# Softplus summed by TensorE in its bank, and one more output product on VectorE, in a fused conv, selective-scan and attention kernel

## The chip, the cores and the metric

The kernel runs on one core of a Trainium2 chip. A core has five engines with in-order instruction streams of their own: TensorE (matmuls into the PSUM banks), VectorE, ScalarE, GpSimd and SyncE, which issues the DMAs here. In the profile they are PE (and PEld, its weight loads), DVE, ACT, POOL and SP. The metric is the device time of one launch in microseconds, the median of several runs.

## What is computed

Eight images of 96 channels and 64 x 64 points go through a layer norm, an input projection, a depthwise convolution, a selective scan over four orders of the points, a gated output projection, a small convolutional branch, linear attention and a quantized feed-forward. Most of the time goes to the selective scan, and the change lies there. Cut to it:

```python
x_dbl = jnp.einsum('bkdl,kcd->bkcl', xs, x_proj_w)             # k: 4 orders, l: 4096 points
dts, bs, cs = (x_dbl[:, :, :R], x_dbl[:, :, R:R + N], x_dbl[:, :, R + N:])   # R = 6, N = 16
dts = jnp.einsum('bkrl,kdr->bkdl', dts, dt_projs_w)            # d: 192 channels
delta = jax.nn.softplus(dts + dt_projs_b[None, :, :, None])
A = -jnp.exp(A_logs)
...
def step(hst, inp):
    u_i, dt_i, b_i, c_i = inp
    dA = jnp.exp(dt_i[..., None] * A)
    hst = dA * hst + (dt_i * u_i)[..., None] * b_i[:, :, None, :]
    y = jnp.einsum('bkdn,bkn->bkd', hst, c_i)
    return (hst, y)
```

For each order, channel d and state n there is a linear recurrence over the 4096 points. `delta` is called the step size.

## The kernel before

**Units.** The scan is cut into 256 units: 8 images x 4 orders x 8 chunks of 512 points, in that order. A unit has six tiles (`TILES`: g in 0, 1 and j in 0 to 2), and each tile has four states (`G`), so 24 slots. In a slot 128 partitions hold 64 channels times two states. The 192 channels are three groups j of 64.

**A slot.** The decay `exp(delta * A)` is made by ScalarE into a PSUM bank (`decays`, three banks of tag "da", two slots ahead). VectorE then runs one scan instruction (L1145) with the decay and the input product as operands, and it starts from the last value that the same state had in the chunk before (`carry`). In a *banked* slot the scan's result goes back to the decay's bank and VectorE multiplies it with C into the tile `hb` (L1147, the product with C); ScalarE copies the last value into `carry` (L1148). In the other slots the scan's result goes to `hb` in place; GpSimd multiplies with C later for all such states of the tile at once (`outputs`, L965), after ScalarE's copy of their last values to `carry` (L1153). `BANKED` tells how many states of each of the six tiles are banked: 4, 0, 4, 0, 4 and then 1 or 2. The first eight units of images 1 to 7 have 1 (13 banked states in the unit), all others 2 (14).

**The inputs.** GpSimd multiplies `b` with `du` = delta x u, a whole tile of 4 x 512 at a time (`inputs`, L959), two tiles ahead of the scan. `b`, `c`, `delta` and `du` are spread from a compact form to the 128 partitions by DMAs on SP (`states`, `spread`).

**The step sizes.** `step_sizes(us, i)` has six steps for one tile `nat` of 128 x 512. Step 0: TensorE forms dts @ dt_w + bias in the single PSUM bank of tag "dt" (L924). Step 1: ScalarE writes the absolute value to `nat` (L932). Step 2: exp(-nat) (L934). Step 3: ln(1 + nat) (L936). Step 4: VectorE adds max(bank, 0) to it (L938), which is the softplus. Step 5: GpSimd multiplies with u, to give du (L941). There are 384 such chains: one for the first 128 channels of each unit (called the a-chain here, 256), and one for the last 64 channels of two units together, in odd units (the pair's or b-chain, 128).

**The sums over states.** TensorE sums the products with C over the states, and the two halves of the partitions, by a matmul with `halves` into the banks "y01" and "y2" (`sums`, L985), adds the skip term or earlier orders by an identity matmul (L994), and ScalarE copies the banks out (`gather`, L1004 and L1007).

**The order.** All engines' streams are written out by hand: `plan` gives for each unit the work put into each of its 24 slots, and every call there appends to the engines' in-order streams in the order of the slots and, inside a slot, of the `put` calls. At the end of each slot one step of the *side streams* may be appended: the front of the next image (normalization, projection, convolution) and the back end of the image before (gating, convolutions, attention, feed-forward). These are generators that yield a number of slots between an operation and the next one that needs its result; `CALM` lists slots in which they may swap ScalarE's function tables.

In `plan`, before: the a-chain of the unit after next has steps 0, 1, 2 in slots 20, 22, 23, and steps 3, 4, 5 follow in slots 0, 2, 4 of the next unit; its spreads are in slots 4 (delta) and 6 (du). The b-chain has steps 0 to 4 in slots 9, 11, 12, 13, 15 and step 5 in slot 16 of odd units, with spreads in slots 17 and 18 (and, for the second unit of the pair, 15 and 16 of the unit after).

Of the kernel before, what the change touches and what calls it, by code (L numbers as in the profile page):

```python
# [12 lines left out]
AF = mybir.ActivationFunctionType  # L13
ALU = mybir.AluOpType
# [7 lines left out]
DI, N, R = 192, 16, 6  # L22
T = 512
NC = L // T
# [6 lines left out]
SPREAD = 5  # L31
HB = 6

BANKED = ((4, 0, 4, 0, 4, 1), (4, 0, 4, 0, 4, 2))

HOLD = 3
LAND = 11
# [6 lines left out]
def kernel(ctx: ExitStack, tc: tile.TileContext, a, out):  # L44
# [8 lines left out]
    nc = tc.nc  # L53
# [9 lines left out]
    def bank(tag, name):  # L63
        return psum.tile([P, T], F32, tag=tag, name=name, bufs=BANKS[tag])


    ident = wp.tile([P, P], F32, name="ident")
# [39 lines left out]
    def into(t, src):  # L107
        nc.sync.dma_start(t, src)
        return t
# [13 lines left out]
    def load(name, shape):  # L123
        return into(wp.tile(shape, F32, name="w_" + name), a[name])
# [26 lines left out]
    dt_w = wp.tile([P, 3, 64], F32, name="dt_w")  # L151
    for k in range(4):
        into(dt_w[32 * k : 32 * k + R], a["dt_w"][:, k, :, 0:64])
        into(dt_w[32 * k + R : 32 * k + R + 1], a["dt_b"][0:64, k, :].rearrange("p j -> j p").unsqueeze(0))
    dt_w = dt_w.rearrange("r j d -> r (j d)")
    a_neg = load("a_logs", [P, 4, 3, 8])
    nc.scalar.activation(a_neg, a_neg, AF.Exp)
# [698 lines left out]
    for b in range(out.shape[0]):  # L856

        s = {"b": b, "done": set(), "live": b + 1 == out.shape[0], "pairs": (1, 0) if b else (0, 1)}
        images.append(s)
        for order, (pair, back) in enumerate((p, k) for p in s["pairs"] for k in range(2)):  # L860
            for i in range(NC):
                u = Unit()
                u.s, u.pair, u.back, u.k = s, pair, back, pair + 2 * back
                u.c, u.start = (NC - 1 - i if back else i), i == 0
                u.order, u.new, u.i = order, (order, i) == (0, 0), len(units)
                u.bc, u.hb, u.delta, u.du = {}, {}, {}, {}
                u.banked = BANKED[int(b == 0 or u.i % 32 >= NC)]
                units.append(u)

    TILES = [(g, j) for g in range(2) for j in range(3)]  # L870
# [32 lines left out]
    def fetched_u(u):  # L903

        u.ua = sp.tile([P, T], F32, tag="ua", name="ua", bufs=1)
        nc.sync.dma_start(u.ua, u.s["u"][u.pair][0:P, bass.ts(u.c, T)])
# [6 lines left out]

    def step_sizes(us, i):

        u, which = us[0], "ab"[len(us) - 1]
        if i == 0:
            u.ps = bank("dt", "dt")
            if which == "a":
                todo = [(u.ps, slice(0, P), u)]  # L920
            else:
                todo = [(u.ps[64 * h : 64 * h + 64], slice(P, DI), w) for h, w in enumerate(us)]
            for ps, d, w in todo:
                nc.tensor.matmul(ps, dt_w[32 * w.k : 32 * w.k + R + 1, d], w.dts, start=True, stop=True)  # L924
            u.nat = sp.tile([P, T], F32, tag="nat" + which, name="nat", bufs=1)
            if which == "a":
                u.nata = u.nat
            else:
                for w in us:
                    w.natb = u.nat  # L930
        elif i == 1:
            nc.scalar.activation(u.nat, u.ps, AF.Abs)  # L932
        elif i == 2:
            nc.scalar.activation(u.nat, u.nat, AF.Exp, scale=-1.0)  # L934
        elif i == 3:
            nc.scalar.activation(u.nat, u.nat, AF.Ln, bias=one)  # L936
        elif i == 4:
            nc.vector.scalar_tensor_tensor(u.nat, u.ps, 0.0, u.nat, ALU.max, ALU.add)  # L938
        else:
            x = u.ua if which == "a" else u.ub  # L940
            nc.gpsimd.tensor_tensor(x, u.nat, x, ALU.mult)  # L941
# [73 lines left out]
    def plan(u, last, nxt, third):  # L1015

        at = [[] for _ in range(24)]

        def put(slot, f, *args):
            at[slot].append((f, args))  # L1020

        if last:
            put(0, outputs, last, 5)
            put(0, before, last)
            for m in range(2):
                put(m, sums, last, (3, 4), 2 + m)
            for m in range(2):
                put(5 + m, sums, last, (5,), m)
            put(7, states, u, 1, 1)
            put(10, gather, last, 0)  # L1030
            put(11, gather, last, 1)
        for n in range(6):
            to = (u, n + 2) if n < 4 else (nxt, n - 4)
            if to[0]:
                put(4 * n + 1, inputs, *to)
        if third and u.i % 2:
            put(16, step_sizes, (nxt, third), 5)
        put(8, outputs, u, 1)
        put(16, outputs, u, 3)
        for m in range(4):  # L1040
            put(13 + m, sums, u, (0, 1), m)
            if m < 2:
                put(18 + m, sums, u, (2,), m)
                put(22 + m, sums, u, (3, 4), m)
        if nxt:
            for i, slot in enumerate((0, 2, 4)):
                put(slot, step_sizes, (nxt,), i + 3)
            put(4, spread, nxt, 0, (0, 1))
            put(6, spread, nxt, 1, (0, 1))
            put(10, states, nxt, 0, 0)  # L1050
            put(15, states, nxt, 1, 0)
            put(20, states, nxt, 0, 1)
            if u.i % 2 == 0:
                put(15, spread, nxt, 0, (2,))
                put(16, spread, nxt, 1, (2,))
        if third:
            put(1, fetched_dt, third)
            put(9, fetched_u, third)
            for i, slot in enumerate((20, 22, 23)):
                put(slot, step_sizes, (third,), i)  # L1060
            if u.i % 2:
                for i, slot in enumerate((9, 11, 12, 13, 15)):
                    put(slot, step_sizes, (nxt, third), i)
                put(17, spread, nxt, 0, (2,))
                put(18, spread, nxt, 1, (2,))
            elif u.i + 3 < len(units):
                put(21, fetched_pair, third, units[u.i + 3])
        return at

    def at_index(i):  # L1070
        return units[i] if 0 <= i < len(units) else None
# [22 lines left out]
    for what in range(2):  # L1094
        spread(units[0], what, range(3))
    fetched_u(units[1])
    for i in range(3):
        step_sizes(units[1:2], i)
    inputs(units[0], 0)
    inputs(units[0], 1)  # L1100
# [9 lines left out]
    for u in units:  # L1110
        last, nxt, third = (at_index(u.i + d) for d in (-1, 1, 2))
        if u.new:
            drained(*side)
            b = u.s["b"]
# [16 lines left out]
        if u.start:  # L1131
            carry = sp.tile([P, 24], F32, tag="carry", name="carry")
        todo = plan(u, last, nxt, third)
        for slot in range(24):
            n, m = divmod(slot, G)
# [6 lines left out]
            d = da.pop(q)  # L1142
# [105 lines left out]
```

## Time and profile before

| what | us |
|---|---|
| median of 3 runs | 11,285.59 |
| lowest and highest run | 11,276.82, 11,286.57 |
| the profiled execution | 11,276.69 |
| its span, first to last instruction | 11,274.7 |
| first scan starts, last scan ends | 299, 11,036 |
| mean of one unit in that stretch | 41.94 |

The costliest groups of that execution:

| line, engine | what | count | mean ns |
|---|---|---|---|
| L959 POOL | input product, 128 x 2048 | 1536 | 4535 |
| L965 POOL | output product, four states | 512 | 4528 |
| L941 POOL | step size times u | 384 | 1279 and 1277 |
| L1145 DVE | scan, 128 x 512 | 6144 | 1204 to 1280 |
| L1147 DVE | product with C, 128 x 512 | 3528 | 692 |
| L938 DVE | softplus sum, 128 x 512 | 384 | 676 |
| L1080 ACT | decay, 128 x 512 | 6144 | 689 |
| L932, L934, L936 ACT | Abs, Exp, Ln of a chain | 384 each | 587, 617, 709 |
| L985 PE | sum over states, records | 12,288 | 724 |
| L924 PE | dt product, records | 1024 | 677 and 647 |

How to read it: a row's mean is one instruction's duration, and neighbours on an engine overlap a little, so the distance from one start to the next is shorter than the sum of durations. A matmul of 32-bit operands shows as two records. An engine's share of busy time averages over stages; which engine sets the pace is read from who waits for whom.

### The profile page before, as it was taken

The page shows a single profiled execution, that of the slowest core. Times are in us where ns is not written, and L with a number is a line of the kernel's source. Part 1 is how long each engine was busy: PE and PEld are TensorE (multiplying, and loading weights), DVE is VectorE, ACT ScalarE, POOL GpSimd, SP SyncE. Part 2 cuts the span into 40 slices and gives each one's busy share as a digit, 9 for nine tenths or more (in the row PEclk, how much of TensorE's full clock was granted, in tenths as well). Part 3 has the DMA queues.
Part 4 walks back from the last instruction along what each step waited for, and adds up shares of the span by engine and source line. Part 5 has one row for each costly group of instructions (what it writes and reads, how often), then busy time and mean ns, then how long its engine had stood idle before and what let it go on. Part 6 is the DMA issues. An engine that isn't in the chain of part 4 may idle for free. (4 is left out here: it accounts for less than half of the span.)

```text
span 11274.7 us, 97032 instructions
## 1 busy us (share of the span) xinstructions
PE 8525.3 (76%) x23270; PEld 2313.7 (21%) x23270; DVE 10391.9 (92%) x10868; ACT 7482.6 (66%) x14899; POOL 10398.6 (92%) x2782
## 2 busy tenths in 40 slices
PE   6677668887788877888678886788767887676677
PEld 1121112222122211222112221222212221111112
DVE  0999999999999999999999999999999999999993
ACT  2666666767666676667766676666766667666674
POOL 0999999999999999999999999999999999999991
PEclk8787778888788877889788887888878887777778
DMA  3788888988888888888888888889888888888883
GB/s 76 195 200 196 200 190 208 215 219 203 199 208 214 217 194 210 208 210 219 195 208 212 213 215 193 217 200 226 209 199 209 213 221 199 194 198 196 202 201 91
DMA packets 1095376, 2253.25 MB, mean 200 GB/s; under 512 B 435993, under 2 KB 436698, under 8 KB 963731
## 3 DMA queue, kind: packets, MB, share of 16 engines
q1 hardware_dynamic: 1094803, 2247.05, 82.1%
q8 instruction: 184, 3.01, 0.1%
q14 instruction: 389, 3.19, 0.1%
HBM read 1507.14 MB, written 336.69 MB: 164 GB/s over the span
## 5 line engine op out<-in xcount | busy, mean ns | idle before, releaser
L959 POOL TENSOR_TENSOR hb<-b,du 128x2048 f32<-128x2048 f32 x1536 | 6938.6, 4535 | 27.0 <-DMA du<-ua 17.0
L1080 ACT ACTIVATE da<-delta,w_a_logs 128x512 f32<-128x512 f32 x6144 | 4216.2, 689 | 693.1 <-DVE hb L1145 570.8
L985 PE MATMUL p<-hb,halves 128*64 128x512 f32 x12288 | 3788.4, 724 | 787.4 <-POOL hb L965 368.5
L1145 DVE TENSOR_TENSOR_SCAN da<-da,carry,hb 128x512 f32<-128x512 f32 x3087 | 3950.2, 1280 | 52.8 <-ACT da L1080 48.9
L965 POOL TENSOR_TENSOR hb<-hb,c 128x2048 f32<-128x2048 f32 (+2 forms) x768 | 2984.6, 3886 | 296.8 <-ACT carry L1153 252.9
L1145 DVE TENSOR_TENSOR_SCAN hb<-da,carry,hb 128x512 f32<-128x512 f32 x2289 | 2781.6, 1265 | 63.6 <-ACT da L1080 62.6
L1147 DVE TENSOR_TENSOR hb<-da,c 128x512 f32<-128x512 f32 x3528 | 2440.8, 692 | 153.9 <-DVE da L1145 0.5
L1148 ACT COPY carry<-da 128x1 f32<-128x1 f32 x3528 | 554.8, 157 | 2337.9 <-DVE hb L1147 2327.3
L985 PEld LDWEIGHTS p<-hb,halves 128*64 128x64 f32 x12288 | 911.3, 161 | 3513.9 <-issue 2095.9
L435 PE MATMUL conv<-f0im,taps 97*128 97x512 f32 (+1 forms) x2088 | 913.0, 670 | 93.3 <-ACT f0pre L491 54.0
L1145 DVE TENSOR_TENSOR_SCAN da<-da,hb 128x512 f32<-128x512 f32 x441 | 537.7, 1219 | 28.3 <-POOL hb L959 27.3
L941 POOL TENSOR_TENSOR ua<-nat,ua 128x512 f32<-128x512 f32 x256 | 327.4, 1279 | 203.0 <-DMA ub<-u 203.0
L924 PE MATMUL dt<-dts,dt_w 7*64 7x512 f32 (+1 forms) x1024 | 451.1, 662 | 15.8 <-DVE nat L938 12.6
L994 PE MATMUL p<-u,ident 128*128 128x512 f32 x768 | 436.2, 695 | 8.8 <-DMA u<-y 8.8
L938 DVE SCALAR_TENSOR_TENSOR nat<-dt,nat 128x512 f32<-128x512 f32 x384 | 259.6, 676 | 184.4 <-ACT nat L936 184.4
L435 PEld LDWEIGHTS conv<-f0im,taps 97*128 97x128 f32 (+1 forms) x2088 | 256.2, 175 | 683.5 <-issue 523.9
L1145 DVE TENSOR_TENSOR_SCAN hb<-da,hb 128x512 f32<-128x512 f32 x327 | 377.9, 1204 | 4.9 <-ACT da L1080 4.9
L376 PE MATMUL ctr<-f1e,cen_c 96*96 96x512 f32 x402 | 234.7, 693 | 137.4 <-DVE f1e L770 98.6
L382 PE MATMUL var<-f1e,ones_c 96*96 96x512 f32 x350 | 210.8, 687 | 146.3 <-ACT f1e L379 131.7
L619 PE MATMUL cab<-f1im,cab_w 97*32 97x512 f32 x1044 | 272.3, 642 | 14.7 <-DVE f1pad L598 7.8
L1153 ACT COPY carry<-hb 128x4 f32<-128x4 f32 (+2 forms) x768 | 146.8, 191 | 196.1 <-DVE hb L1145 184.1
L656 PE MATMUL cab<-f1m,cab_w 96*96 96x512 f32 x348 | 205.2, 717 | 93.1 <-ACT f1e L665 42.1
(427 smaller groups left out, 7512.6 us busy)
## 6 DMA issues: line engine op xcount, KB each, us to landing
b<-xd SPq DMA_DIRECT2D x1024, 512.0 KB
c<-xd SPq DMA_DIRECT2D x1024, 512.0 KB
delta<-nat SPq DMA_DIRECT2D x1536, 128.0 KB
du<-ua SPq DMA_DIRECT2D x1024, 128.0 KB
y<-yt SPq DMA_DIRECT2D x512, 256.0 KB
u<-y SPq DMA_DIRECT2D x384, 256.0 KB
ua<-u SPq DMA_DIRECT2D x256, 256.0 KB
du<-ub SPq DMA_DIRECT2D x512, 128.0 KB
```

The lines of the kernel that those rows point to most:

```text
L435: nc.tensor.matmul(ps, taps[:, t, lo : lo + n], im[:, r0 + dy : r0 + dy + 8, dx : dx + HW], start=t == 0, stop=t == 8,)
L619: nc.tensor.matmul(ps[at : at + 32, :], cab1_w[:, t, :], k.im.t[:, 8 * q + dy : 8 * q + dy + 8, dx : dx + HW], start=t == 0, stop=t == 8, ...
L924: nc.tensor.matmul(ps, dt_w[32 * w.k : 32 * w.k + R + 1, d], w.dts, start=True, stop=True)
L941: nc.gpsimd.tensor_tensor(x, u.nat, x, ALU.mult)
L959: nc.gpsimd.tensor_tensor(hb, u.bc[0, g], u.du[j].unsqueeze(1).to_broadcast([P, G, T]), ALU.mult)
L965: nc.gpsimd.tensor_tensor(hb, hb, u.bc[1, TILES[n][0]][:, lo:, :], ALU.mult)
L985: nc.tensor.matmul(ps, halves, u.hb[n][:, i, :], start=TILES[n][0] == 0 and m == 0, stop=False, skip_group_check=True)
L994: nc.tensor.matmul(ps, w, x, start=False, stop=True, skip_group_check=True)
L1080: nc.scalar.activation(da[q], u.delta[j], AF.Exp, scale=a_neg[:, u.k, j, g * G + m : g * G + m + 1])
L1145: nc.vector.tensor_tensor_scan(dd if banked else x, dd, x, 0.0 if u.start else col, ALU.mult, ALU.add)
L1147: nc.vector.tensor_tensor(hb[:, m, :], d, u.bc[1, g][:, m, :], ALU.mult)
L1148: kept.append(lambda col=col, d=d, at=first_at: nc.scalar.copy(col, d[:, at : at + 1]))
```

## The change

The chain's bank holds half of the pre-activation, since `dt_w` (weights and bias) is scaled by 0.5 at the start. After the absolute value, TensorE adds `nat` to the bank by an identity matmul, so that the bank holds max(x, 0). The exponential takes a scale of -2. After the logarithm TensorE adds `nat` again, and the bank holds the softplus; ScalarE copies it to `nat` in step 4, which was VectorE's. `BANKED` becomes 2 for the first eight units of images 1 to 7 and for all even units, and 3 for the other odd units: 14 or 15 banked states. The steps are put into other slots: of the a-chain, 0 and 1 into slots 18 and 20, 2 to 5 into slots 0, 1, 3, 5 of the next unit, spreads 5 and 7; of the b-chain, 0 to 4 into slots 7, 8, 10, 11, 16, step 5 into 17, spreads 18 and 19.

```diff
-BANKED = ((4, 0, 4, 0, 4, 1), (4, 0, 4, 0, 4, 2))
+BANKED = ((4, 0, 4, 0, 4, 2), (4, 0, 4, 0, 4, 3))
...
+        half_w = dt_w[32 * k : 32 * k + R + 1]
+        nc.vector.tensor_scalar(half_w, half_w, 0.5, None, ALU.mult)
...
-                u.banked = BANKED[int(b == 0 or u.i % 32 >= NC)]
+                u.banked = BANKED[u.i % 2 if b == 0 or u.i % 32 >= NC else 0]
...
+        def added():
+            nc.tensor.matmul(u.ps, ident, u.nat, start=False, stop=True, skip_group_check=True)
...
         elif i == 1:
             nc.scalar.activation(u.nat, u.ps, AF.Abs)
+            added()
         elif i == 2:
-            nc.scalar.activation(u.nat, u.nat, AF.Exp, scale=-1.0)
+            nc.scalar.activation(u.nat, u.nat, AF.Exp, scale=-2.0)
         elif i == 3:
             nc.scalar.activation(u.nat, u.nat, AF.Ln, bias=one)
+            added()
         elif i == 4:
-            nc.vector.scalar_tensor_tensor(u.nat, u.ps, 0.0, u.nat, ALU.max, ALU.add)
+            nc.scalar.copy(u.nat, u.ps)
...
+        if nxt:
+            for i, slot in ((2, 0), (3, 1), (4, 3), (5, 5)):
+                put(slot, step_sizes, (nxt,), i)
+        if third and u.i % 2:
+            put(17, step_sizes, (nxt, third), 5)
...
-        if third and u.i % 2:
-            put(16, step_sizes, (nxt, third), 5)
...
-            for i, slot in enumerate((0, 2, 4)):
-                put(slot, step_sizes, (nxt,), i + 3)
-            put(4, spread, nxt, 0, (0, 1))
-            put(6, spread, nxt, 1, (0, 1))
+            put(5, spread, nxt, 0, (0, 1))
+            put(7, spread, nxt, 1, (0, 1))
...
-            for i, slot in enumerate((20, 22, 23)):
+            for i, slot in enumerate((18, 20)):
                 put(slot, step_sizes, (third,), i)
             if u.i % 2:
-                for i, slot in enumerate((9, 11, 12, 13, 15)):
+                for i, slot in enumerate((7, 8, 10, 11, 16)):
                     put(slot, step_sizes, (nxt, third), i)
-                put(17, spread, nxt, 0, (2,))
-                put(18, spread, nxt, 1, (2,))
+                put(18, spread, nxt, 0, (2,))
+                put(19, spread, nxt, 1, (2,))
...
-    for i in range(3):
+    for i in range(2):
         step_sizes(units[1:2], i)
```

More of the change, by code (lines that the diff above doesn't have):

```diff
@@ L923, in step_sizes @@
             for ps, d, w in todo:
-                nc.tensor.matmul(ps, dt_w[32 * w.k : 32 * w.k + R + 1, d], w.dts, start=True, stop=True)
+                nc.tensor.matmul(
+                    ps, dt_w[32 * w.k : 32 * w.k + R + 1, d], w.dts, start=True, stop=True, skip_group_check=True
+                )
             u.nat = sp.tile([P, T], F32, tag="nat" + which, name="nat", bufs=1)
```

## The prediction

> **What bounds the kernel now.** I read the busy shares first, then the shares by stretch, then the waits of the two busiest engines, then single instructions in order of time. The chain that ended last adds up to only a few per cent of the span, so it names no bound here. The page:
>
> ```profile
> PE 8525.3 (76%) x23270; PEld 2313.7 (21%) x23270; DVE 10391.9 (92%) x10868; ACT 7482.6 (66%) x14899; POOL 10398.6 (92%) x2782
> ```
>
> VectorE and GpSimd tie at 92%, start and end included. The two stretches below are image 0 and images 1 to 7 of the scan loop (stretch, length, then PE, PEld, DVE, ACT, POOL busy with counts, granted clock, DMA share, GB/s).
>
> ```profile
> 300.00:1590.00 1290.00, 888.32 (x2348) 240.48 (x2350) 1250.69 (x1271) 818.48 (x1648) 1278.03 (x336) 0.78 0.82 196
> 1590.00:11030.00 9440.00, 7281.56 (x19989) 1952.99 (x19986) 9058.60 (x9422) 6483.37 (x12977) 9092.94 (x2412) 0.83 0.85 207
> ```
>
> In image 0 GpSimd is busy 99%, VectorE 97%; in the rest both are at 96%. The waits between 450 and 10,900 us decide between them (us in total, times, longest):
>
> ```profile
> DVE hb L1145 <- ACT da L1080: 67.5, 93, 3.0
> DVE da L1145 <- ACT da L1080: 48.9, 22, 6.4
> ...
> DVE f1ln L719 <- ACT var L370: 24.2, 22, 2.7
> ...
> DVE da L1145 <- POOL hb L959: 4.9, 7, 1.2
> ```
>
> ```profile
> POOL hb L965 <- ACT carry L1153: 233.7, 193, 4.3
> POOL ub L941 <- DVE nat L938: 51.7, 38, 3.2
> ```
>
> VectorE waits 4.9 us for GpSimd; GpSimd waits 233.7 us for carry copies, which themselves wait for the last scan of a tile. So VectorE sets the pace after image 0, and GpSimd is close behind. VectorE's other stalls are late decays: ScalarE is in order, and a decay stuck behind other work holds a scan up.
>
> **What one instruction is worth on VectorE** is a distance between starts, not a duration:
>
> ```profile
> 5019.84 1.23 DVE L1145 TENSOR_TENSOR_SCAN hb<-da,hb 128x512 f32<-128x512 f32 x1 [0.76 <-ACT da L1080]
> 5020.98 1.27 DVE L1145 TENSOR_TENSOR_SCAN da<-da,carry,hb 128x512 f32<-128x512 f32 x1
> 5022.33 0.69 DVE L1147 TENSOR_TENSOR hb<-da,c 128x512 f32<-128x512 f32 x1
> 5022.94 1.28 DVE L1145 TENSOR_TENSOR_SCAN da<-da,carry,hb 128x512 f32<-128x512 f32 x1
> ...
> 5026.79 0.68 DVE L938 SCALAR_TENSOR_TENSOR nat<-dt,nat 128x512 f32<-128x512 f32 x1
> 5027.39 1.28 DVE L1145 TENSOR_TENSOR_SCAN da<-da,carry,hb 128x512 f32<-128x512 f32 x1
> ```
>
> A slot with the product takes 1.96 us here, and the softplus sum adds 0.60 (5026.79 to 5027.39). Over all 6144 scans the mean from scan to scan is 1.942 us with a product, 1.210 without; with a softplus sum between, 2.527 and 1.785. So a product costs 0.73 us and a softplus sum 0.58. As a test: 3528 x 1.942 + 2616 x 1.210 + 384 x 0.58 = 10,240 us of a loop of 10,737 (first scan 299, last end 11,036); the other 500 are the side streams' products and their stalls.
>
> **The change on VectorE.** Removed: 384 softplus sums (L938) x 0.58 = 223 us. Added: products. Before, 56 units had 13 and 200 had 14 (3528). After, the 56 have 14, 100 even ones 14, 100 odd ones 15: 3684, so 156 more x 0.73 = 114 us. Net 109 us less, all on the pacing engine, about 0.85 us per pair of units. Four tiny scalings of dt_w run at the start, where VectorE is busy 17.9 of the first 200 us: nothing; if that cover were gone, four small instructions, under 2 us.
>
> **On GpSimd.** The output product of the last tile loses one state 156 times. The rows:
>
> ```profile
> L965 POOL TENSOR_TENSOR hb<-hb,c 128x1024 f32<-128x1024 f32 x200 | 473.0, 2365 | 111.4 <-ACT carry L1153 95.3 <-DMA ub<-u 4.3 <-DMA x1d<-f1e 3.2
> L965 POOL TENSOR_TENSOR hb<-hb,c 128x1536 f32<-128x1536 f32 x56 | 193.1, 3447 | 7.5 <-DMA u<-u 3.7 <-ACT carry L1153 3.0
> ```
>
> A state is 3447 - 2365 = 1.08 us, so 168 us less. That is more than VectorE's 109, so GpSimd does not take over. In image 0, where it is full, it gives back 16 x 1.08 = 17 us against VectorE's 16 x 1.03 = 16 (3 x 0.58 - 0.73 per pair). Against this, step 5 (the product with u, one per chain) now waits for ScalarE's copy in slot 3 instead of VectorE's sum in slot 2. GpSimd began it in slot 3 in 138 of 256 units; the copy ends some 1.45 us into slot 3 (carry 0.16 + decay 0.69 + copy 0.58), the sum ended just as it began. At worst 138 x 1.4 = 190 us of new GpSimd wait, at best none; images 1 to 7 have 9440 - 9093 = 347 us of GpSimd idle time to hide it, so I take 8 us. The pair's product moves past one output product (slot 16 to 17), and its two du transfers from slot 18 to 19; their first reader is in slot 1 of the next unit, 6 slots on. The a-chain's four delta and four du issues go from slots 4 and 6 to 5 and 7 on SP; their readers are in slots 17 and 22. SP already waits there (on nat, 1917 us in all) without holding anyone: nothing; if the cover went, the next issue behind them (b, c) has 5 slots.
>
> **On ScalarE** each chain gains one copy out of the bank, and each matmul chain two adds on TensorE. The nearest rows:
>
> ```profile
> L1007 ACT COPY yt<-p 128x512 f32<-128x512 f32 x368 | 212.5, 578 | 6.6 <-PE p L994 6.6
> L994 PE MATMUL p<-u,ident 128*128 128x512 f32 x768 | 436.2, 695 | 8.8 <-DMA u<-y 8.8
> ```
>
> Copies: 384 x 0.578 = 222 us, ScalarE from 66 to 69%. It lies beside VectorE as long as decays stay ahead. From the times in the trace, a decay ends 1.1 to 3.5 us (medians by slot) before its scan, except in odd units' slots 14 and 15, where it is 0.4: there the pair's chain runs its Exp and Ln in slots of 1.2 us. Slots 13 to 16 of odd units run 0.63 us over their medians, 128 x 0.63 = 80 us. The change moves this chain to slots 8, 10, 11 and 16, where a slot lasts 1.9 us, and the other chain's Abs and Exp from 22 and 23 to 20 and 0. The stall of decays may thus shrink, at most by those 80 us.
>
> **On TensorE**, 384 x 2 adds by the identity, two records each. L994 is the same shape: in order of time a lone pair of such records takes 1.10 us (four take 1.98), so 768 x 1.10 = 845 us at most, 768 x 0.99 = 760 in a row; the share goes from 76 to about 83%. No term of the path, but three waits are new: the add waits for Abs (or Ln) and holds every later matmul, the side streams' and sums among them; Exp waits until the add has read nat; the copy waits for the second add. Behind Exp and the copy on ScalarE stand the decays. From Abs to Exp there are 4 slots (a-chain) or 2 (b-chain), from Ln to the copy 2 or 5. ScalarE's cover is the lead above; bounds: nothing, and 2 x 1.10 x 384 = 845 us if every one were felt. With 180 us of ScalarE waiting for TensorE in the loop today over more than a thousand hand-overs, I take 5 to 10% of 845, about 60, and against it most of the 80 of the emptied slots: zero for both together, ends -70 and +60.
>
> [...] Here waits on TensorE reach 11 us, and the granted clock was 0.78 in image 0 and 0.83 in the busier rest. [...]
>
> **Sum.** The profiled execution took 11,276.7 us (span 11,274.7). 11,276.7 - 109 + 8 + 0 = 11,176; the median of the three runs is 8.9 above that execution, so 11,185 us, -0.9%. Its own range, from -70 to +60: 11,115 to 11,245.
>
> **Rivals.**
> *More than that (0.12).* The 80 us of odd slots 13 to 16 vanish and TensorE costs nothing: 11,185 - 75 = 11,110. For it: the 0.4 us lead there. Against: even units, with no pair chain, run over in the same slots too.
> *GpSimd keeps half (0.10).* It waits for the copy in every unit where it came early and falls behind: of the 190 us a third shows, 11,185 + 55 = 11,240. For: 99% in image 0. Against: 347 us of idle time later.
> *It does nothing, within 0.2% (0.08).* The 109 us are eaten by late decays, 11,285.
> *Slower (0.20).* ScalarE in order: Exp in slots 0 and 10, Abs in 8 (one slot after its matmul, where there were two) and the copy in slots 3 and 16 wait for a TensorE that is itself held by the adds, and decays come late. Priced 845 us times the share VectorE feels; it decides from (109 - 8) / 845 = 12%, and at a fifth it is 169 us: 11,354. For: 83% TensorE, an odd unit with five such ScalarE steps besides the decays in slots 8 to 11. Against: TensorE began the dt product slots ahead of its place in half the units.
>
> **How the numbers follow.** Forecast 0.50. What a measurement here can tell from no change is about 0.2%, 23 us. Faster: 0.50 + 0.12 + 0.10 = 0.72; same 0.08; slower 0.20. From 11,090 (5% below) to 11,320 (a share of 16% felt, some 12% above).
>
> **What would show it.** No VectorE row of nat; L1147's row at 3684, VectorE's scan to scan at 1.94 and 1.21 as now; GpSimd 168 us less busy; "DVE L1145 <- ACT da" not above 180 us; odd slots 13 to 16 shorter. Wrong if ScalarE's waits for PE dt exceed 100 us, or VectorE's for ScalarE double.

## The result, and the profile after

The changed kernel takes 11,366.82 us (median of four runs, 11,366.36 to 11,383.9) against 11,282.42 for the kernel before on the same chip: a ratio of 1.0079, 95% interval 1.0061 to 1.0096. It is 84 us slower where 100 us faster was forecast, and outside the range; the rival "Slower" had named 11,354. The profiled execution took 11,367.25 us, its span is 11,365.5.

The page's row of busy times:

```profile
PE 9025.4 (79%) x24806; PEld 2505.5 (22%) x24806; DVE 10279.0 (90%) x10644; ACT 7712.2 (68%) x15439; POOL 10235.4 (90%) x2782
```

The two engines that tied have both less to do: VectorE 113 us less than before, GpSimd 163. So the work went away as forecast, and the time went up. The two stretches of the scan loop (stretch, length, PE, PEld, DVE, ACT, POOL busy with counts, granted clock, DMA share, GB/s) show where:

```profile
300.00:1590.00 1290.00, 942.12 (x2545) 258.75 (x2544) 1238.01 (x1242) 855.64 (x1721) 1269.18 (x337) 0.83 0.82 196
1590.00:11110.00 9520.00, 7707.29 (x21316) 2119.49 (x21312) 8951.57 (x9216) 6672.93 (x13437) 8939.64 (x2411) 0.87 0.84 205
```

In images 1 to 7 VectorE and GpSimd fell from 96% to 94% each: neither is full, and something else holds both up. Image 0 became 8.7 us shorter (1292.9 to 1284.2 from first scan to first scan of image 1); the loss is in the rest. The waits between 450 and 11,000 us (us in total, times, longest) name it:

```profile
PE dt L924 <- ACT nat L944: 598.6, 206, 8.9
PE dt L924 <- ACT nat L949: 370.7, 173, 7.7
PE dt L924 <- ACT carry L1163: 329.9, 117, 8.0
...
ACT nat L944 <- PE dt L934: 184.6, 88, 9.0
DVE hb L1160 <- ACT da L1095: 96.4, 133, 2.8
DVE da L1160 <- ACT da L1095: 93.1, 53, 6.1
...
ACT nat L952 <- PE dt L924: 18.2, 23, 2.8
...
DVE da L1160 <- POOL hb L973: 1.1, 3, 0.5
```

L924 is the add, L934 the dt product, L944 Abs, L947 Exp, L949 Ln, L952 the copy, L1160 the scan, L1095 the decay. TensorE stands before its adds for 1,300 us, waiting for Abs or Ln (a carry copy, L1163, is named where it was the last thing on ScalarE to signal). Such a wait of TensorE before an add is called a hold below. ScalarE's Abs now waits 185 us for the dt product; before it was this:

```profile
ACT nat L932 <- PE dt L924: 2.7, 2, 2.0
```

Most of that comes from the new slots and not from the adds: a kernel below with the new slots and no add has 146.5 us of it. VectorE's waits for decays went from 116 to 190 us. GpSimd does not pace it: VectorE waits 1.1 us for it. The same in groups of instructions (count, then busy and mean ns, then idle time before them and its releasers):

```profile
L924 PE MATMUL dt<-nat,ident 128*128 128x512 f32 x1536 | 1097.0, 803 | 1348.1 <-ACT nat L944 611.6 <-ACT nat L949 383.4 <-ACT carry L1163 343.9
L944 ACT ACTIVATE nat<-dt 128x512 f32<-128x512 f32 x384 | 223.9, 583 | 208.7 <-PE dt L934 196.3 <-DMA delta<-nat 11.7 <-DMA b<-xd 0.2
L947 ACT ACTIVATE nat<-nat 128x512 f32<-128x512 f32 x384 | 237.8, 619 | 5.2 <-PE dt L924 5.1
L952 ACT COPY nat<-dt 128x512 f32<-128x512 f32 x384 | 222.0, 578 | 25.5 <-PE dt L924 25.0
L1162 DVE TENSOR_TENSOR hb<-da,c 128x512 f32<-128x512 f32 x3684 | 2547.7, 692 | 181.6 <-DMA c<-xd 12.5 <-DVE da L1160 1.8 <-issue 0.9
```

Of the new hand-overs that the forecast named, Exp (5.1 us) and the copy (25 us) hardly wait; the adds do. VectorE's product now waits 12.5 us for the transfer of c. One stretch of an odd unit shows a whole chain. First TensorE in order of time (start, duration, engine, line, operation; in brackets the idle time before it and its releaser):

```profile
6680.67 1.02 PE L924 MATMUL dt<-nat,ident 128*128 128x512 f32 x2
6681.53 1.02 PE L437 MATMUL conv<-f0im,taps 97*128 97x512 f32 x2
6682.40 0.38 PE L781 MATMUL ff<-f1x,q_w 96*128 96x512 fp8e5 x1
6682.61 1.02 PE L437 MATMUL conv<-f0im,taps 97*128 97x512 f32 x2
6689.69 2.07 PE L924 MATMUL dt<-nat,ident 128*128 128x512 f32 x2 [6.05 <-ACT carry L1163]
6691.56 1.91 PE L437 MATMUL conv<-f0im,taps 97*128 97x512 f32 x2
6693.40 1.97 PE L999 MATMUL p<-hb,halves 128*64 128x512 f32 x4
6695.30 0.39 PE L781 MATMUL ff<-f1x,q_w 96*128 96x512 fp8e5 x1
```

Then ScalarE, and VectorE:

```profile
6687.81 0.69 ACT L1095 ACTIVATE da<-delta,w_a_logs 128x512 f32<-128x512 f32 x1 [2.96 <-DVE hb L1160]
...
6688.92 0.72 ACT L949 ACTIVATE nat<-nat,one 128x512 f32<-128x512 f32 x1
...
6691.45 1.90 ACT L1095 ACTIVATE da<-delta,w_a_logs 128x512 f32<-128x512 f32 x3
6695.73 0.58 ACT L789 CAST f1h<-ff 128x512 f16<-128x512 f32 x1 [2.38 <-PE ff L781]
...
6697.63 0.69 ACT L1095 ACTIVATE da<-delta,w_a_logs 128x512 f32<-128x512 f32 x1
```

```profile
6696.64 0.69 DVE L1162 TENSOR_TENSOR hb<-da,c 128x512 f32<-128x512 f32 x1
6698.35 1.29 DVE L1160 TENSOR_TENSOR_SCAN da<-da,carry,hb 128x512 f32<-128x512 f32 x1 [1.02 <-ACT da L1095]
```

The pair's second add reaches the head of TensorE's stream at 6683.6 and stands there for 6.05 us, until Ln ends on ScalarE (6688.92 + 0.72). Ln itself is that late because it stands behind a decay that waits 2.96 us for a scan. Nothing behind the add passes it. The convolution, the sums and a feed-forward matmul (L781) follow, the add and the first of these in about twice the time (2.07 and 1.91 us where the same pairs took 1.02). ScalarE comes to the copy of that feed-forward bank and waits 2.38 us; the decay behind it comes late, and a scan waits 1.02 us. ScalarE holds TensorE, TensorE holds ScalarE, and VectorE pays.

How much it pays can be counted: idle gaps of VectorE over 60 ns in images 1 to 7 add up to 458 us before and 647 after (both hold about 175 behind the last scan). The 189 more are 14 in even units and 175 in odd ones, which have the pair's chain. By what the profile names as their end, 81 of them stand before scans and 61 before VectorE's other steps, both for ScalarE, 19 for TensorE and 17 for a transfer: late decays are less than half, and the side streams' steps most of the rest. With the forecast's -109 that makes +80; measured was +84.

### The profile page after: what moved, and what is told of

The parts are those of the page before. It is cut to its first block, busy times and chain, and to the rows that moved or that the text cites. A ratio compares the mean times of both kernels' runs of the same rounds, so it can differ in the third digit from the quotient of the medians.

```text
span 11365.5 us, 99689 instructions
## 1 busy us (share of the span) xinstructions
PE 9025.4 (79%) x24806; PEld 2505.5 (22%) x24806; DVE 10279.0 (90%) x10644; ACT 7712.2 (68%) x15439; POOL 10235.4 (90%) x2782
## 5 line engine op out<-in xcount | busy, mean ns | idle before, releaser
L1095 ACT ACTIVATE da<-delta,w_a_logs 128x512 f32<-128x512 f32 x6144 | 4208.1, 690 | 790.8 <-DVE hb L1160 667.3
L1160 DVE TENSOR_TENSOR_SCAN da<-da,carry,hb 128x512 f32<-128x512 f32 x3236 | 4138.8, 1279 | 99.5 <-ACT da L1095 96.9
L999 PE MATMUL p<-hb,halves 128*64 128x512 f32 x12288 | 3540.8, 683 | 224.3 <-ACT yt L1021 128.0
L979 POOL TENSOR_TENSOR hb<-hb,c 128x2048 f32<-128x2048 f32 (+2 forms) x768 | 2818.2, 3670 | 408.8 <-ACT carry L1168 327.8
L1162 DVE TENSOR_TENSOR hb<-da,c 128x512 f32<-128x512 f32 x3684 | 2547.7, 692 | 181.6 <-DMA c<-xd 12.5
L1160 DVE TENSOR_TENSOR_SCAN hb<-da,carry,hb 128x512 f32<-128x512 f32 x2140 | 2608.9, 1265 | 90.2 <-ACT da L1095 82.5
L924 PE MATMUL dt<-nat,ident 128*128 128x512 f32 x1536 | 1097.0, 803 | 1348.1 <-ACT nat L944 611.6
L1163 ACT COPY carry<-da 128x1 f32<-128x1 f32 x3684 | 577.6, 157 | 1706.6 <-DVE hb L1162 1697.0
L999 PEld LDWEIGHTS p<-hb,halves 128*64 128x64 f32 x12288 | 843.1, 153 | 2755.6 <-issue 2023.2
L1160 DVE TENSOR_TENSOR_SCAN da<-da,hb 128x512 f32<-128x512 f32 x448 | 546.2, 1219 | 214.8 <-POOL hb L973 213.6
L924 PEld LDWEIGHTS dt<-nat,ident 128*128 128x128 f32 x1536 | 279.9, 225 | 1996.0 <-ACT nat L944 831.6
L934 PE MATMUL dt<-dts,dt_w 7*64 7x512 f32 (+1 forms) x1024 | 430.2, 634 | 4.8 <-DMA dts<-xd 3.1
L1008 PE MATMUL p<-u,ident 128*128 128x512 f32 x768 | 395.2, 637 | 14.0 <-DMA u<-y 13.9
L1160 DVE TENSOR_TENSOR_SCAN hb<-da,hb 128x512 f32<-128x512 f32 x320 | 371.1, 1204 | 15.1 <-ACT da L1095 15.1
L944 ACT ACTIVATE nat<-dt 128x512 f32<-128x512 f32 x384 | 223.9, 583 | 208.7 <-PE dt L934 196.3
```

Of the source, the lines that this page charges most:

```text
L924: nc.tensor.matmul(u.ps, ident, u.nat, start=False, stop=True, skip_group_check=True)
L979: nc.gpsimd.tensor_tensor(hb, hb, u.bc[1, TILES[n][0]][:, lo:, :], ALU.mult)
L999: nc.tensor.matmul(ps, halves, u.hb[n][:, i, :], start=TILES[n][0] == 0 and m == 0, stop=False, skip_group_check=True)
L1008: nc.tensor.matmul(ps, w, x, start=False, stop=True, skip_group_check=True)
L1095: nc.scalar.activation(da[q], u.delta[j], AF.Exp, scale=a_neg[:, u.k, j, g * G + m : g * G + m + 1])
L1160: nc.vector.tensor_tensor_scan(dd if banked else x, dd, x, 0.0 if u.start else col, ALU.mult, ALU.add)
```

## The experiments

"Stalls" below is that sum of gaps in images 1 to 7 of the profiled execution. Line numbers shift by some lines from kernel to kernel; the names in front of them tell the operation. Times before are those of the same chip, between 11,282.67 and 11,287.0.

**The banked products alone.** The first kernel is the changed one with the old BANKED, the second the kernel before with the new one.

```diff
-BANKED = ((4, 0, 4, 0, 4, 2), (4, 0, 4, 0, 4, 3))
+BANKED = ((4, 0, 4, 0, 4, 1), (4, 0, 4, 0, 4, 2))
```

> The changed kernel with the old BANKED (13 or 14 banked states), adds, copy and slots as changed. Theory 1 (the lost time comes with the adds: ScalarE waits for a late TensorE, decays come late): only the 156 products leave VectorE, 156 x 0.73 = 114 us, so 11,367 - 114 = 11,253 us, up to 11,283 if GpSimd, which gets 168 us back, starts to pace; Abs still waits for TensorE about 185 us. Theory 2 (odd units lose because of their 15th product): its stalls of some 194 us go as well, 11,060 to 11,110.

> The kernel before with the new BANKED alone (14 or 15), its softplus sum on VectorE. Theory 1: VectorE gets 156 products, 114 us, and no further stalls: 11,282 + 114 = 11,396 us. Theory 2: the stalls of about 194 us come too: 11,590.

Measured: 11,299.48 (ratio 1.0015, 1.0006 to 1.0025) and 11,413.45 (1.0114, 1.0099 to 1.0129). Without the products the changed kernel's odd units stall as long (500.5 us against 498.8) and Abs waits as long (184.5), so the third product of odd units is not what broke. The products cost 131 us in the kernel before, near their 114, and only 67 came back when they were taken out of the changed one: there GpSimd had its 10,398 us again, and VectorE's waits for it (450 to 10,900 us) rose from 1.1 to 52.0 us.

**TensorE's load.** The adds are made one column wide, and ScalarE's copy becomes an exponential of the same shape (ScalarE is busy 7,706 us in all against 7,712); everything waits as it did.

```diff
-            nc.tensor.matmul(u.ps, ident, u.nat, ...)
+            nc.tensor.matmul(u.ps[:, 0:1], ident, u.nat[:, 0:1], ...)
...
-            nc.scalar.copy(u.nat, u.ps)
+            nc.scalar.activation(u.nat, u.ps, AF.Exp)
```

> The changed kernel with each add one column wide (so the sum is right in the first column alone; the copy out is an exponential, to keep the step sizes positive). All waits between ScalarE and TensorE stay, TensorE's load of the adds goes. If TensorE's load makes it late: VectorE's extra stalls of 194 us go, 11,170 to 11,230, and Abs waits for the dt product less than 60 us. If the order (the add holding later matmuls until Abs or Ln has run) does it: 11,367 within 25, with Abs still waiting some 185 us.

Measured: 11,382.38 (1.0091, 1.0076 to 1.0106), stalls 661.7. The adds' records fell from 803 to 292 ns, the idle time before them rose to 1,493 us, Abs waited 200.0 us, and nothing was gained. TensorE's busy time fell by only 270 us, from 9,025 to 8,756, because the granted clock fell as well (0.865 to 0.831) and a sum's record rose from 683 to 722 ns; so the load was lowered, not taken away. With that limit, it isn't the columns that the adds stream, and what is left is that they wait in TensorE's order.

**Abs later.** The pair's Abs, Exp and Ln go to slots 10, 11 and 12; its dt product stays in slot 7.

```diff
-                for i, slot in enumerate((7, 8, 10, 11, 16)):
+                for i, slot in enumerate((7, 10, 11, 12, 16)):
```

> The changed kernel with the pair's Abs, Exp and Ln in slots 10, 11 and 12 and not in 8, 10 and 11; its dt product stays in 7, its copy in 16. If the place of Abs, one slot behind its matmul, is the cause: ScalarE's waits for the dt product fall from 185 us below 60, VectorE's stalls in odd units' slots 10 to 13 fall by some 90 us, 11,275. If TensorE is late in any slot, or Exp and Ln in shorter slots give it back: above 11,340.

Measured: 11,458.42 (1.0159, 1.0142 to 1.0176), 92 us above the changed kernel: a miss. The waits of that kernel:

```profile
PE dt L924 <- ACT nat L944: 698.3, 230, 9.0
...
DVE hb L1160 <- ACT da L1095: 163.9, 197, 4.8
...
ACT nat L944 <- PE dt L934: 21.3, 18, 4.3
```

Abs no longer waits (21.3 us), and the stall in odd units' slot 10 went from 60.7 to 7.4. But the adds follow Abs and Ln, so TensorE stood 100 us longer before Abs, and slots 12, 14 and 18 stalled 35, 21 and 32 us more. So taking Abs's wait away gave nothing back; Exp and Ln stand in shorter slots here as well, which this run does not separate.

**Adds later in TensorE's stream.** Each add is put one or two slots behind its Abs or Ln, so that other matmuls go first; ScalarE's steps stay where they are.

```diff
         elif i == 1:
             nc.scalar.activation(u.nat, u.ps, AF.Abs)
-            added()
+        elif i == 6 or i == 7:
+            nc.tensor.matmul(u.ps, ident, u.nat, ...)
...
-            for i, slot in ((2, 0), (3, 1), (4, 3), (5, 5)):
+            for i, slot in ((2, 0), (3, 1), (7, 2), (4, 3), (5, 5)):
...
-            for i, slot in enumerate((18, 20)):
+            for i, slot in ((0, 18), (1, 20), (6, 22)):
...
-                for i, slot in enumerate((7, 8, 10, 11, 16)):
+                for i, slot in ((0, 7), (1, 8), (6, 9), (2, 10), (3, 11), (7, 13), (4, 16)):
```

> The changed kernel with each add moved later in TensorE's stream, so that its operand is ready when TensorE gets there: the a-chain's from slots 20 and 1 to 22 and 2, the pair's from 8 and 11 to 9 and 13; all ScalarE steps stay. If TensorE held by the adds is the cause: its idle time before the adds falls from 1,300 us below 600, VectorE's stalls by some 100 us, 11,230 to 11,300. If only Abs one slot behind the dt product matters, or ScalarE's own load: 11,367 within 25.

Measured: 11,283.09 against 11,287.0 (0.9997, 0.9987 to 1.0006), 84 us less than the changed kernel. Its group of adds, and two of its waits:

```profile
L944 PE MATMUL dt<-nat,ident 128*128 128x512 f32 x1536 | 1027.2, 755 | 597.4 <-ACT nat L948 275.0 <-ACT carry L1161 170.6 <-ACT nat L942 147.3
```

```profile
ACT nat L942 <- PE dt L932: 199.2, 90, 5.8
...
ACT nat L946 <- PE dt L944: 28.8, 23, 3.3
```

The idle time before the adds fell from 1,348 to 597 us, the stalls from 647 to 572.4. Nothing but the place of a chain's two adds in TensorE's stream was changed, so the hold is a cause, worth these 75 us. In odd units, where VectorE's other steps waited 157 us for ScalarE and TensorE, they now wait 98 (82 before the change). The stalls before scans did not move: 126 us in odd units in both kernels, 56 before. So the hold reached VectorE mostly through the side streams, and the late decays are not explained by it. Abs still waits, too.

**The pair's product earlier as well.** The same with the pair's dt product in slot 5 instead of 7, so that it can't be late for Abs; then also with the old BANKED.

```diff
-                for i, slot in ((0, 7), (1, 8), (6, 9), ...
+                for i, slot in ((0, 5), (1, 8), (6, 9), ...
```

> The run with the later adds, and besides the pair's dt product in slot 5 and not in 7, three slots ahead of its Abs. If the rest of the loss (Abs still waited 199 us for that product) comes from the product standing one slot ahead of its reader: Abs waits less than 60 us, odd units' stalls in slots 9 to 12 fall from 121 to about 50, 11,190 to 11,230. If TensorE is late there whatever the place: 11,283 within 15.

> The same with the old BANKED. VectorE loses 114 us of products; the changed kernel gained 67 from this, GpSimd taking the rest. So 67 to 114 below the run before it: 11,080 to 11,150; if GpSimd paces (10,398 us busy, as in the run with the direct softplus at 11,105), not below 11,105.

Measured: 11,418.12 (1.0111, 1.0094 to 1.0128) and 11,305.73 (1.0018, 1.0008 to 1.0027). A miss: 135 us more than with the product in slot 7. The waits of the first:

```profile
DVE hb L1158 <- ACT da L1093: 179.7, 206, 10.7
...
ACT nat L946 <- PE dt L944: 117.1, 50, 7.2
ACT var L371 <- PE var L384: 68.5, 35, 5.0
...
ACT nat L942 <- PE dt L932: 32.9, 29, 3.5
...
PE dt L932 <- DMA dts<-xd: 47.7, 17, 5.4
...
PE dt L932 <- ACT nat L950: 32.2, 28, 1.6
...
PE dt L932 <- ACT carry L1161: 17.8, 7, 4.2
```

Abs waits 33 us instead of 199, but Exp now waits 117 us for the add (29 with the product in slot 7), and the side streams' norms (L371) 68 us (24). Stalls are 677.5, with slots 9, 11 and 12 of odd units at 59.8, 48.2 and 73.0. TensorE is still late in that part of the odd unit, and ScalarE meets it one hand-over further on, nearer to the short slots 12 to 15. One reason shows in the last three lines: in its earlier place the product itself holds TensorE, for its transfer of dts and for the copy (L950) out of the single dt bank, 97 us where it was 1.0 us in slot 7, and the holds before the adds rose from 597 to 710 us. So this was a second hold, and no test of Abs's wait alone. With the old BANKED the kernel gained 112 us, as expected of the products, and stayed slower than the one before the change.

**Which chain, and is it the slots?** In the first kernel the pair's chain is as before (VectorE's sum, old slots) and the a-chain keeps its adds; the second has no adds and no copy at all, but all the new slots and BANKED.

```diff
         elif i == 1:
             nc.scalar.activation(u.nat, u.ps, AF.Abs)
-            added()
+            if which == "a":
+                added()
...
-            nc.scalar.copy(u.nat, u.ps)
+            if which == "a":
+                nc.scalar.copy(u.nat, u.ps)
+            else:
+                nc.vector.scalar_tensor_tensor(u.nat, u.ps, 0.0, u.nat, ALU.max, ALU.add)
...
-                for i, slot in enumerate((7, 8, 10, 11, 16)):
+                for i, slot in enumerate((9, 11, 12, 13, 15)):
```

> The changed kernel with the pair's chain (128 of 384) as before the change: slots 9, 11, 12, 13, 15, 16, its sum on VectorE and no adds; the a-chain keeps adds and copy. If the pair's adds make the stalls of odd units' slots 10 to 13 and 16: VectorE gets 128 x 0.58 = 74 us back and loses some 120 us of stalls, 11,320. If the a-chain's adds make them: 11,367 + 74 = 11,440.

> The slots and BANKED of the changed kernel with the softplus sum on VectorE, so without adds and copy. If the adds make the stalls: the kernel before plus 156 products, 11,282 + 114 = 11,396, near 11,413 of the run with the new BANKED alone. If the new slots make them (Abs one slot after its matmul, more ScalarE work in the calm slots): 11,367 + 223 = 11,590.

Measured: 11,286.85 against 11,287.0 (0.9999, 0.999 to 1.0008), stalls 487.6; and 11,431.98 (1.0129, 1.0114 to 1.0144), stalls 490.8. Waits of the second:

```profile
ACT nat L942 <- PE dt L932: 146.5, 63, 5.9
...
DVE hb L1156 <- ACT da L1091: 66.3, 94, 2.0
DVE da L1156 <- ACT da L1091: 45.0, 21, 4.0
```

The first shows that 256 of the 384 chains have their adds for 29 us of stalls, although TensorE still idles 960 us before them; the 128 of the pair, with their new slots, make the other 160. In the second, Abs waits 146.5 us for its product without any add, and VectorE waits no longer for decays than before (111 us against 116). So the slots make most of Abs's wait, and they alone cost little (with the caveat that its VectorE has 223 us more to do, which gives the decays more time). Where the hold falls decides, not how long it is in all.

**No hand-over at all.** The kernel before with the softplus as ln(1 + exp(x)): two steps on ScalarE and none elsewhere (it leaves out the protection of large x); then with the new BANKED too.

```diff
         elif i == 1:
-            nc.scalar.activation(u.nat, u.ps, AF.Abs)
+            nc.scalar.activation(u.nat, u.ps, AF.Exp)
         elif i == 2:
-            nc.scalar.activation(u.nat, u.nat, AF.Exp, scale=-1.0)
-        elif i == 3:
             nc.scalar.activation(u.nat, u.nat, AF.Ln, bias=one)
-        elif i == 4:
-            nc.vector.scalar_tensor_tensor(u.nat, u.ps, 0.0, u.nat, ALU.max, ALU.add)
+        elif i < 5:
+            pass
```

> The kernel before with the softplus as ln(1 + exp(x)) in two ScalarE steps (without the protection of large x that the absolute value gives), no sum on VectorE, no adds. If VectorE's work and its hand-overs are all that counts: 11,282 - 223 = 11,059, with a little less for the missing Abs. If GpSimd takes over, whose 10,398 us stay: its stalls in the loop, some 340 us, can be eaten at most, 11,100 to 11,200.

> The direct softplus with the new BANKED: 156 products from GpSimd (168 us) to VectorE (114 us). With the old one GpSimd is busy 98% of the loop. If it alone paced: faster than 11,105. If VectorE paces again: 11,282 - 109 = 11,173, the sum of the prediction without any add.

Measured: 11,104.88 (0.984, 0.9823 to 0.9856) and 11,203.3 (0.9928, 0.9911 to 0.9945). The second has on VectorE exactly the change that was forecast at -109, and gained 82 with 29 us of new stalls. The first gained 182 of 223. Its windows, and its VectorE's waits for GpSimd between 450 and 10,900 us:

```profile
300.00:1590.00 1290.00, 905.62 (x2360) 238.88 (x2360) 1233.75 (x1231) 799.70 (x1615) 1288.86 (x339) 0.79 0.84 198
1590.00:10860.00 9270.00, 7254.52 (x19979) 1961.28 (x19976) 8855.90 (x9080) 6305.65 (x12632) 9077.16 (x2410) 0.84 0.87 211
```

```profile
DVE da L1143 <- POOL hb L957: 29.6, 38, 1.9
```

GpSimd (the fifth pair) is busy 1288.86 of 1290 us in image 0 and 98% afterwards. VectorE waits 29.6 us for it where it was 4.9, and image 0 became 14 us shorter where its 48 sums are 28; together that is most of the missing 41, so a nearly full GpSimd fits them. But it does not set the pace: with 156 products taken off it, the second kernel is 98 us slower, not faster. In each of the five pairs of kernels here that differ in BANKED alone, the one with more products on VectorE is slower, by 131, 67, 98, 112 and 73 us. The change's second half was a loss wherever it was tried.

**The best of these on the full computation.** The a-chain with adds, the pair's chain as before, and the old BANKED.

> The kernel before with one change: the a-chain (256 chains) has its softplus summed by TensorE and copied by ScalarE, in the slots of the changed kernel; the pair's chain keeps VectorE's sum and its old slots, and BANKED is the old one (13 or 14 products). On VectorE this takes away 256 x 0.58 = 148 us and adds nothing. Theory, that the harm comes from the pair's adds and the a-chain's cost about 30 us of late decays (487.6 against 458 of stalls with the same chains and the new BANKED): 148 - 30 = 118 us less than before, some 11,167, unless GpSimd, back at 10,398 us of work, takes over on the way; with GpSimd full at 98 to 99.9% the direct softplus ran at 11,105, so there is room: 11,150 to 11,190, VectorE's stalls 470 to 500. First rival, that each handover to TensorE costs alike: a third of the pair's harm and more is with the a-chain as soon as VectorE has slack to lose, and the time stays within 11,250 to 11,290, as the changed kernel with the old BANKED did (11,299). Second rival, GpSimd paces: it is over 97% busy in the loop, VectorE's waits for it rise above 15 us, and only about half shows, 11,205 to 11,230.

Measured: 11,213.38 against 11,286.02 (0.9936, 0.9923 to 0.995), stalls 515.6: 73 us faster than before and 153 faster than the changed kernel, and 46 above the expectation. Two of its waits:

```profile
DVE hb L1165 <- ACT da L1100: 98.4, 131, 4.1
...
DVE da L1165 <- POOL hb L978: 25.7, 32, 1.9
```

VectorE waits 25.7 us for GpSimd (4.9 before), which is busy 99% in image 0 and 97% later. The theory's sign and the second rival's size held. Part of the gain goes to GpSimd; of the 57 us of new stalls, though, GpSimd ended 16 and ScalarE 42.

**The account.** VectorE's own work at the forecast's prices (0.58 us a softplus sum, 0.73 a product), the stalls beyond the 458 of before, their sum, and the measured difference, all in us:

| kernel | work | stalls | sum | measured |
|---|---|---|---|---|
| the changed kernel | -109 | +189 | +80 | +84 |
| old BANKED | -223 | +198 | -25 | +17 |
| before, new BANKED | +114 | +12 | +126 | +131 |
| thin adds | -109 | +203 | +94 | +100 |
| Abs late | -109 | +245 | +136 | +176 |
| adds deferred | -109 | +114 | +5 | -4 |
| and product early | -109 | +219 | +110 | +133 |
| and old BANKED | -223 | +226 | +3 | +20 |
| adds in the a-chain only | -34 | +29 | -5 | 0 |
| no adds, new slots | +114 | +33 | +147 | +145 |
| direct softplus | -223 | +32 | -191 | -182 |
| and new BANKED | -109 | +29 | -80 | -82 |
| a-chain only, old BANKED | -148 | +57 | -91 | -73 |

Eleven of thirteen sums lie within 23 us of the measurement, the other two within 42. The stalls are those of one execution, the measured times are medians: with the old BANKED, for example, the ten runs lie between 11,284.03 and 11,330.47 us and the profiled one took 11,284.8. The table is bookkeeping of VectorE's time: it shows that the prices were right and that the stalls are what differs, not what makes them. They are large only where the pair's chain has adds.

## Why the prediction was wrong

- *VectorE, -109.* Right: 113 us less busy, 3684 rows of the product, and -82 in the direct softplus with the new BANKED, which has this change on VectorE without adds (and one step less on ScalarE).
- *GpSimd, -168 and +8.* Right in size (163 less), and the wait for the copy held nobody: VectorE waits 1.1 us for GpSimd.
- *ScalarE, +222.* Right: 230 more.
- *TensorE, at most 845.* Mis-sized: the adds are busy 1,097 us, since 803 ns is the mean record instead of 0.55 us each in a pair; many start after a hold, and a pair then took 2.07 us (median, after 4 us or more) where it took 1.12 after none. TensorE's share rose to 79% and not to 83, and its other matmuls became faster (a sum's record 683 ns where it was 724). The thin adds, which lowered its load by 270 us, gained nothing.
- **The step that failed is "zero for both together, ends -70 and +60"** for the decays, "5 to 10% of 845, about 60, and against it most of the 80 of the emptied slots". It was +189, 22% of 845, three times the upper end. Two parts of it fell. The share was taken from the waits of ScalarE for TensorE before the change, 180 us over a thousand hand-overs, as if new hand-overs behaved like old ones; but an add that waits in TensorE's stream delays every other reader of TensorE. ScalarE's waits for TensorE outside the softplus chain, from the first scan of image 1 to the last scan, went from 180 to 270 us, and to 158 with the adds deferred. And the relief did not come: odd units' slots 13 to 16 stall 42 us before and 81 after. The runs show where the 189 lie, and part of why: 160 go when the pair's chain loses its adds and new slots, the new slots alone make 33, and 75 go when the adds stand later in TensorE's stream.
- *The rival "Slower"* had the right sign, with a chance of 0.20, and nearly the price (a fifth, 11,354; measured 22%, 11,367). Its TensorE "held by the adds" is shown. Its way to VectorE is not: of the five ScalarE waits it named, Exp and the copy are 5 and 25 us, and Abs, the one that is long, waits nearly as long with no add at all and costs little there. The shown part went through the side streams' banks, as in the stretch above, which no part of the forecast priced. That a fifth came so near is in part luck.
- *The lead* that spoke against it ("TensorE began the dt product slots ahead of its place in half the units") did not move with the product. Counted by the scans that VectorE has started, the pair's product begins in slot 9 in the median before, its place, and in slot 8 after, one behind its new place 7, with or without adds; Abs follows one slot later instead of two.
- *SyncE, nothing.* Too little: VectorE's waits for the transfer of c are 12 to 18 us in all ten kernels with the new slots, and at most 2.3 in the others. No run separates which of the moved transfers does it.
- *The clock.* The sum had no term for it, in either direction. In images 1 to 7 the granted clock rose from 0.83 to 0.87 and a sum's record fell from 724 to 683 ns. But a pair of add records takes 1.12 us (median) after no idle time, 1.34 after 2 to 3 us and 2.07 after 4 us or more. Of 768 pairs 238 took over 1.8 us, 225 us more of TensorE than at 1.12. The pairs turn over between 2 and 4 us: over 1.8 us are 26 of 69 after 2 to 3 us, 52 of 71 after 3 to 4, and 121 of 125 beyond. So the mean record of a sum became shorter, while a pair behind a long hold takes nearly twice as long as one behind none. What of the 189 us belongs to these slower pairs, and what to the hold itself, no run here separates.
- *Its own signs.* The forecast was to be wrong if ScalarE's waits for the dt bank passed 100 us; they are 203. The kernel with the new slots and no adds has 146.5 and few new stalls, so this sign was no good measure of the harm. VectorE's waits for decays are 190, above its 180.

What stays open is the rest of the deferred kernel: 114 us of stalls over those of before are left, 112 of them in odd units, 71 of these before scans. Abs's wait of 199 us, the copies on ScalarE and the pair's new slots all stand in that kernel, and no run separates them; deferred adds with the pair's Abs in a later slot were not tried.

## What to carry to other kernels

A matmul that needs another engine's result, put right behind it in TensorE's stream, blocks every later matmul for as long as that engine takes to come round to it (1,348 us before the adds here, up to 8.9 us at a time); price it by who waits for those later matmuls, and put it a few places down the stream (75 us of stalls less here), or leave it out where the in-order engine it waits for also waits for TensorE. A lead that a trace shows at one place need not move along when the instruction is moved (here the pair's product was put two slots earlier in the stream, and began one earlier). A long wait is not yet a cost: Abs's was 146.5 us in a kernel with 33 us of new stalls, and 21.3 in one with 245. When two engines tie, ask which of them waits for the other before moving work between them: here VectorE waited at most 52 us for GpSimd, and output products moved to it cost time in all five pairs.

## What was not expected of the hardware

The mean granted clock was higher in the kernels with adds (0.855 to 0.871) than in those without (0.825 to 0.834) and than with one-column adds (0.831, with as many matmuls): it went with the columns streamed, although the adds come with holds of up to 9 us. From first to last scan TensorE idles for more than 4 us 215 times before and 176 times after, 1,316 and 997 us in all: many of the long gaps of before are gone, and the holds before the adds are new ones (124 of the 176, 658 us).
